# Moving the other weights and inputs behind the first query product of an attention and mixture-of-experts layer, and sharing its tail with GpSimd

## The chip, the core and the metric

The kernel runs on one core of one Trainium2 chip, as one launch. The metric is the device time of an execution in microseconds (us). Before the change, six runs have a median of 538.36 us (535.7 to 539.39). The engines have these names here: PE (TensorE, matrix products), DVE (VectorE), ACT (ScalarE), POOL (GpSimd), SP (SyncE, which here only issues DMAs). ACT and POOL issue DMAs as well. PE and DVE work from and into SBUF, and into PSUM banks, of which there are eight.

## The reference

The input is x, 8 sequences of 512 tokens of 128 numbers, all in fp32. One layer of attention and one of experts are computed, each with a residual and a layer norm behind it:

```python
Q = x @ Wq.T + bq;  K = x @ Wk.T + bk;  V = x @ Wv.T + bv        # 16 heads of 8
scores = einsum('bnqd,bnkd->bnqk', Q, K) / sqrt(128), causal
attn = softmax(scores);  out = (attn @ V) @ Wo.T + bo
x = layernorm(x + out)
probs = softmax(x @ gate_w.T)                                    # 14 experts
w, i = top_2(probs);  w = w / sum(w)
moe = sum over the two: w * (gelu(x @ w1[i] + b1[i]) @ w2[i] + b2[i])
x = layernorm(x + clip(x + moe, -100, 100))
```

## The kernel before, in words

**Loads and constants (lines 90 to 216).** ACT issues the four projection weights (L92), then the query and key biases in eight small DMAs, 32 numbers each (L106), then the value and output bias, the gate, b1, b2 and six rows of -1 for the key tiles (L109 to L208). SP issues all eight sequences of x, 256 KB each (L95). POOL writes the constants: the identity, masks, counters, the value buffers `v_aug` (2 x 128x2048 zeros, L196), `w_all`. DVE casts the counters to fp32 (L166).

**Small products (L293 to L324).** PE turns the four weights, the gate, the value bias and b1 over; DVE copies them to SBUF. From them come the output bias with the value bias folded in (`bo_bc`), and the gate folded into the value and output weights (`wvX`, `woX`), with its bias and sum.

**Attention as a pipeline of steps.** A sequence has four units of four heads, a unit has five steps. In step s, `front` makes a block of 1024 scores on PE and DVE takes its row maxima (L463, L468, L475); `back`, twelve steps behind (LAG), makes the scores again with the maximum taken off, ACT takes their exponential, POOL or PE masks them, and `product` multiplies by the values. Scores use the bf16 pieces of q and k (three pieces each), which `split` makes: a product on PE, a piece on ACT, the rest on DVE (`qrest`, `krest`), the other pieces, a store to DRAM, and `load_rows` reads them back into a ring of tiles. Three PSUM tiles (`ps_u`) hold scores; the other products share two banks (`ps_m`) in order of use.

All other work hangs in a list by step: `at(step, fn, ...)`. Within a step the order is back, front, then the list in the order in which it was filled. Each engine carries out its instructions in the program's order. Sequence b starts at step 20(b - 1): `load_xT` (x turned over), five and six steps later `split` for q and k, fifteen later `values` (L347). What would lie before step 0 stands in step -1: for sequence 0 these are `load_xT`, both splits, `values` and four `load_rows`.

**Routing and experts.** Tokens are scattered by expert to DRAM (`XS`), the experts' blocks run through PE, and their rows are scattered to `OS`. `biases` puts the first terms, b2 by routing weight and the residual y, into `acc` (which is x_sb).

**The tail (L1242 to L1294).** For each of eight chunks (four tiles of 128 tokens) `gather` loads both experts' rows from OS (one DMA on SP, one on ACT, six chunks ahead); `add_up` adds acc and the two by three products with the identity into one of the two `ps_m` banks; `residual_2` on DVE clips (L1263), adds y (L1264) and takes each tile's mean and variance (L220, L221, eight instructions); `layernorm_scale` on POOL makes the scale by a power (L228 to L231); `store`, two chunks later, applies scale and shift in four ACT instructions and issues one DMA on SP.

Of the kernel before, what the change touches and what calls it, by code (L numbers as in the profile page):

```python
# [8 lines left out]
FP = mybir.dt.float32  # L9
AF = mybir.ActivationFunctionType  # L10
ALU = mybir.AluOpType
# [25 lines left out]
def kernel(  # L37
# [56 lines left out]
    for b in range(B):  # L94
        nc.sync.dma_start(x_sb[:, b * NQ : (b + 1) * NQ, :], x_v[:, b * NQ : (b + 1) * NQ, :])  # L95

    ident = const.tile([P, P], FP, tag="ident", name="ident")
    make_identity(nc, ident)

    bias_q = const.tile([P, 1], FP, tag="bias_q", name="bias_q")  # L100
    bias_k = const.tile([P, 1], FP, tag="bias_k", name="bias_k")
    with nc.allow_non_contiguous_dma(reason="128 biases, one to a partition"):
        for src, dst in ((bq, bias_q), (bk, bias_k)):
            src_v = src.rearrange("(g j d) -> g d j", j=GH, d=HD)
            for g in range(NG):
                nc.scalar.dma_start(dst[g * P // NG : (g + 1) * P // NG], src_v[g])  # L106
    bv_bc = const.tile([P, D], FP, tag="bv_bc", name="bv_bc")
    bo_bc = const.tile([P, D], FP, tag="bo_bc", name="bo_bc")
    nc.scalar.dma_start(bv_bc, bv.partition_broadcast(P))  # L109
    nc.scalar.dma_start(bo_bc, bo.partition_broadcast(P))  # L110

    gate_nat = const.tile([E, D], FP, tag="gate_nat", name="gate_nat")
    nc.scalar.dma_start(gate_nat, gate_w)
    b1_nat = const.tile([E * NFC, P], FP, tag="b1_nat", name="b1_nat")
    nc.scalar.dma_start(b1_nat, b1.rearrange("e (c f) -> (e c) f", f=P))
    b2_blk = const.tile([P, NQ, D], FP, tag="b2_blk", name="b2_blk")
    nc.gpsimd.memset(b2_blk, 0.0)
    for t in range(NQ):
        nc.scalar.dma_start(b2_blk[HS * t : HS * t + E, t, :], b2)
# [41 lines left out]

    def counting(name, shape, pattern, base, mult):
        raw = const.tile([P] + shape, I32, tag=f"{name}_i", name=f"{name}_i")
        nc.gpsimd.iota(raw, pattern=pattern, base=base, channel_multiplier=mult)
        dst = const.tile([P] + shape, FP, tag=name, name=name)
        nc.vector.tensor_copy(dst, raw)  # L166
        return dst
# [8 lines left out]
    nc.vector.tensor_copy(place, base_e)  # L176
# [16 lines left out]
    v_aug, qr, kr = [], [], []  # L193
    for i in range(2):
        va = const.tile([P, NQ, HEADS, HS], FP, tag=f"v_aug{i}", name=f"v_aug{i}")
        nc.gpsimd.memset(va, 0.0)  # L196
        nc.gpsimd.memset(va[:, :, :, HD : HD + 1], 1.0)
        v_aug.append(va)
    minus = const.tile([PC, GH, T], BF, tag="minus", name="minus")
    nc.vector.memset(minus, -1.0)  # L200


    ring = const.tile([P, RING, 2, GH, T], BF, tag="ring", name="ring")
    for i in range(RING):
        at = (i - NU % RING) % RING
        qr.append(ring[0:KS, at, 0])
        kr.append(ring[0:KS, at, 1])
        nc.scalar.dma_start(kr[i][KR:KS], minus)  # L208
# [4 lines left out]
    nc.gpsimd.tensor_copy(y_sb[:, :, D + 1], ids[:, 0, :])  # L213
    stats = const.tile([P, NT, 2], FP, tag="stats", name="stats")
    w_all = const.tile([P, NT, HS], FP, tag="w_all", name="w_all")
    nc.gpsimd.memset(w_all, 0.0)

# [55 lines left out]
    with tc.tile_pool(name="work", bufs=2) as work, tc.tile_pool(  # L273
# [20 lines left out]
        for i in range(4):  # L294
            nc.tensor.transpose(wt[:, i * P : (i + 1) * P], wnat[:, i, :], ident)
        for i, dst in enumerate((wqT, wkT)):

            nc.vector.tensor_copy(
                dst.rearrange("p (g d j) -> p g d j", j=GH, d=HD),
                wt[:, i * P : (i + 1) * P].rearrange("p (g j d) -> p g d j", j=GH, d=HD),  # L300
            )
        for i, dst in ((2, wvT), (3, woT)):
            nc.vector.tensor_copy(dst, wt[:, i * P : (i + 1) * P])
        gt = bank("gt")
        nc.tensor.transpose(gt[:, 0:E], gate_nat, ident[:E, :E])
        nc.vector.tensor_copy(gateT, gt[:, 0:E])

        bo_t = bank("bo_t")
        nc.tensor.transpose(bo_t[:, 0:P], bv_bc, ident)
        bvT = work.tile([P, T], FP, tag="num", name="bvT")[:, 0:P]  # L310
        nc.vector.tensor_copy(bvT, bo_t[:, 0:P])
        nc.tensor.matmul(bo_t[:, P : 2 * P], bvT, woT, start=True, stop=True)
        nc.vector.tensor_tensor(bo_bc, bo_bc, bo_t[:, P : 2 * P], ALU.add)
        nc.tensor.transpose(bo_t[:, 2 * P : 3 * P], bo_bc, ident)
        boT = work.tile([P, T], FP, tag="num", name="boT")[:, 0:P]
        nc.vector.tensor_copy(boT, bo_t[:, 2 * P : 3 * P])
        gp = bank("gp")
        for i, w in enumerate((wnat[:, 3, :], boT, ones)):
            nc.tensor.matmul(gp[:, i * P : i * P + E], w, gateT, start=True, stop=True)
        for i, dst in enumerate((woX[:, D:], gate_bias, gate_sum)):  # L320
            nc.vector.tensor_copy(dst, gp[:, i * P : i * P + E])
        bt = bank("bt")
        nc.tensor.transpose(bt[:, 0 : E * NFC], b1_nat, ident[: E * NFC, : E * NFC])
        nc.vector.tensor_copy(b1T, bt[:, 0 : E * NFC])  # L324
# [655 lines left out]
        for b in range(B):  # L980

            s0 = (b - 1) * BSTEP
            at(max(s0, -1), load_xT, b)
            for n, (w, bias, nm) in enumerate(((wqT, bias_q, "q"), (wkT, bias_k, "k"))):
                step = max(s0 + 5 + n, -1)
                at(step, split, step, b, w, bias, nm)
            at(max(s0 + 15, -1), values, b)
            for g in range(NG):
                u = b * NG + g


                at(max(step_of(u - RING, UN) + LAG, s0 + (10, 13, 15, 18)[g], -1), load_rows, u)
# [260 lines left out]

        def add_up(c):
            sums[c] = bank(f"sum_{c}").rearrange("p (t d) -> p t d", d=D)
            parts = acc[:, c * NQ : (c + 1) * NQ, :], *got.pop(c)
            for i, part in enumerate(parts):
                nc.tensor.matmul(sums[c], ident, part, start=(i == 0), stop=(i == 2))

        def residual_2(c):  # L1260
            ts = slice(c * NQ, (c + 1) * NQ)
            z = z_sb[:, ts, :]
            nc.vector.tensor_scalar(z, sums.pop(c), CLIP, -CLIP, ALU.min, ALU.max)  # L1263
            nc.vector.tensor_tensor(z, z, y_sb[:, ts, 0:D], ALU.add)  # L1264
            for i in range(NQ):
                layernorm_stats(ffn, z_sb[:, c * NQ + i, :], c * NQ + i)
            scales[c] = layernorm_scale(ffn, c, 1)

        def store(c):
            rstd, shift = scales.pop(c)  # L1270
            for i in range(NQ):
                t = c * NQ + i
                nc.scalar.activation(
                    z_sb[:, t, :],
                    z_sb[:, t, :],
                    AF.Identity,
                    bias=shift[:, i : i + 1],
                    scale=rstd[:, i : i + 1],
                )
            ts = slice(c * NQ, (c + 1) * NQ)  # L1280
            nc.sync.dma_start(out_v[:, ts, :], z_sb[:, ts, :])

        inner.close()
        ffn = inner.enter_context(tc.tile_pool(name="tail", bufs=3, reuse_waits="tile"))
        for c in range(6):
            gather(c)
        for c in range(B + 2):
            if c < B:
                add_up(c)
                residual_2(c)  # L1290
                if c + 6 < B:
                    gather(c + 6)
            if c >= 2:
                store(c - 2)  # L1294

# [42 lines left out]
```

## Time and profile before

| | us |
|---|---|
| median of six runs | 538.36 |
| profiled execution, device time | 539.48 |
| its span, first to last instruction | 537.8 |
| first query product starts | 20.22 |
| first scores start | 36.07 |
| last expert product ends | about 491.4 |
| first gather issued / first sum with it starts | 498.40 / 502.12 |
| last statistics end / last ACT instruction ends | 530.83 / 534.51 |

Over the span PE is busy 84%, DVE 71%, POOL 60%, ACT 57%; the mean granted PE clock is 0.944 of full speed.

The profile has several views. The page gives busy shares and the costliest groups of instructions. The *timeline* lists instructions in order of time: start, length, engine, line of the kernel, operation, output <- inputs with their shapes, and in brackets how long the engine was idle before and who released it. The *chain of waits* starts from the last instruction and goes back at each step to what released it: start, length, what. The *windows* give the busy time of each engine, the granted PE clock and the DMA rate in stretches of time.

### The profile page before, as it was taken

To read this page: it belongs to the slowest core of one execution; us is meant where nothing else is said; L and a number is where in the kernel's file an instruction comes from. 1 tells how busy PE (TensorE), PEld (TensorE's weight loads), DVE (VectorE), ACT (ScalarE), POOL (GpSimd) and SP (SyncE) were. 2 spreads that over 40 slices of the span, in tenths; PEclk is the share of its full clock that TensorE was granted. 3 is DMA by queue.
4 is the path that set the end of the run, shared out by engine and by line. 5 is a ranking of instruction groups with operands and counts; after the bars stand their busy time and mean duration, and the time that the engine had idled before them with its cause. 6 is when DMAs were issued, how large, how long until landed. Compare 5 with 4: busy or idle time off the path is not lost.

```text
span 537.8 us, 10861 instructions
## 1 busy us (share of the span) xinstructions
PE 449.2 (84%) x3367; PEld 277.2 (52%) x3367; DVE 379.9 (71%) x932; ACT 306.9 (57%) x512; POOL 322.8 (60%) x678
## 2 busy tenths in 40 slices
PE   1737999999999999989999988959867999886690
PEld 0424555555555555545555554526656887774240
DVE  4219668669879878878878889982576665663394
ACT  0302567667766866866866756556554465572054
POOL 6001334453588578578578578676477777777143
PEclk9968699999999999999999999998988999999696
DMA  7144322442443443553443433345155333331952
GB/s 188 36 140 126 104 97 100 135 148 98 141 158 132 141 158 103 153 166 132 143 152 131 142 107 100 101 125 141 34 163 152 107 94 89 89 96 33 243 149 78
DMA packets 66740, 66.23 MB, mean 123 GB/s; under 512 B 10861, under 2 KB 55382, under 8 KB 66683
## 3 DMA queue, kind: packets, MB, share of 16 engines
q1 hardware_dynamic: 55008, 53.26, 33.4%
q0 software_dynamic: 4512, 8.47, 4.7%
q10 hardware_dynamic: 7162, 3.81, 2.6%
q8 instruction: 27, 0.44, 0.4%
q14 instruction: 31, 0.25, 0.2%
HBM read 37.75 MB, written 26.05 MB: 119 GB/s over the span
## 4 chain that ended last, share of the span: by engine, by line
PE 49%; DVE 17%; ACT 11%; POOL 8%; issue 7%; DMA 6%; ACTq 1%; SPq 1%; POOLq 0%; DVEq 0%
PE av L587 12%; PE f L423 7%; PE b L509 7%; ACT pt L563 6%; PE h L1102 5%; PE o L1119 5%; PE f L433 3%; POOL pt L520 3%; DVE mx L463 2%; ACT oT L597 2%; POOL OS L243 2%; DVE mx L468 2%; POOL XS L243 2%; PE bp L1177 1%; DVE ob L1127 1%
## 5 line engine op out<-in xcount | busy, mean ns | idle before, releaser
L563 ACT ACTIVATE pt<-b 128x1024 f32<-128x1024 f32 x160 | 163.0, 1021 | 42.4 <-PE b L509 34.9
L520 POOL TENSOR_SCALAR_AFFINE_SELECT pt<-pt 128x256 f32<-128x256 f32 (+1 forms) x210 | 91.2, 450 | 72.9 <-ACT pt L563 72.2
L423 PE MATMUL f<-ring 72*128 72x384 bf16 (+3 forms) x512 | 114.4, 307 | 18.0 <-DMA ring<-qsc 9.4
L509 PE MATMUL b<-ring 75*128 75x384 bf16 (+3 forms) x512 | 100.7, 308 | 6.2 <-ACT pt L563 3.4
L475 DVE TENSOR_REDUCE mx<-f 128x2 f32<-128x1024 f32 x64 | 78.1, 1223 | 29.0 <-PE f L433 27.9
L243 POOL DMA_INDIRECT OS<-ob,bto_i x77 | 75.1, 975 | 28.7 <-DVE ob L1127 9.7
L587 PE MATMUL av<-pt,v_aug 128*32 128x512 f32 (+3 forms) x1024 | 84.0, 439 | 5.6 <-POOL pt L520 4.9
L433 PE MATMUL f<-causal_bf,ident_bf 128*128 128x256 bf16 (+1 forms) x320 | 82.6, 258 | 0.0
L468 DVE TENSOR_REDUCE mx<-f 128x8 f32<-128x1024 f32 x64 | 77.1, 1213 | 5.5 <-PE f L433 5.2
L423 PEld LDWEIGHTS <-ring 72*128 72x128 bf16 x512 | 50.7, 100 | 52.0 <-issue 28.3
L509 PEld LDWEIGHTS <-ring 75*128 75x128 bf16 x512 | 42.5, 100 | 39.4 <-issue 26.4
L1107 ACT ACTIVATE hT<-h,wt 128x256 f32<-128x256 f32 (+1 forms) x92 | 35.3, 437 | 35.3 <-PE h L1102 35.1
L587 PEld LDWEIGHTS av<-pt,v_aug 128*32 128x32 f32 x1024 | 27.2, 109 | 52.2 <-issue 37.2
L463 DVE TENSOR_REDUCE mx<-f 128x4 f32<-128x1024 f32 x32 | 39.1, 1222 | 14.5 <-PE f L433 12.2
L1102 PE MATMUL h<-bxT,wt 128*128 128x256 f32 (+1 forms) x184 | 44.1, 365 | 5.5 <-DVE begins L873 3.2
L1119 PE MATMUL o<-wt,hT 128*128 128x128 f32 x308 | 44.0, 284 | 1.3 <-ACT hT L1107 1.3
L1119 PEld LDWEIGHTS o<-wt,hT 128*128 128x128 f32 x308 | 42.2, 199 | 4.2 <-ACT hT L1107 2.1
L433 PEld LDWEIGHTS <-ident_bf 128*128 128x128 bf16 x320 | 31.8, 99 | 14.8 <-issue 2.3
L1127 DVE TENSOR_SCALAR ob<-o,bxb 128x128 f32<-128x128 f32 x77 | 24.0, 347 | 20.3 <-PE o L1119 18.1
L243 POOL DMA_INDIRECT XS<-second,to_i x32 | 32.6, 1020 | 8.9 <-issue 8.9
L243 POOL DMA_INDIRECT XS<-y_sb,to_i x32 | 32.3, 1010 | 9.4 <-issue 5.3
L1102 PEld LDWEIGHTS h<-bxT,wt 128*128 128x128 f32 x184 | 30.5, 199 | 11.1 <-ACT wt L1074 5.2
(215 smaller groups left out, 625.0 us busy)
## 6 DMA issues: line engine op xcount, KB each, us to landing
ring<-ksc SPq DMA_DIRECT2D x32, 288.0 KB
ring<-qsc SPq DMA_DIRECT2D x96, 96.0 KB
osc<-oT SPq DMA_DIRECT2D x24, 256.0 KB
bxb<-XS SPq DMA_DIRECT2D x31, 130.0 KB
ring<-in_L_ffn_w_dram SPq DMA_DIRECT2D x28, 128.0 KB
qsc<-qpc SPq DMA_DIRECT2D x24, 128.0 KB
ksc<-kpc SPq DMA_DIRECT2D x24, 128.0 KB
x_sb<-in_L_attn_x_dram SPq DMA_DIRECT2D x8, 256.0 KB
```

The costliest lines, as they stand in the source:

```text
L243: inst = nc.gpsimd.indirect_dma_start(dst, bass.IndirectOffsetOnAxis(ap=idx, axis=0), src, None, bounds_check=bound, oob_is_err=False,)
L423: nc.tensor.matmul(ps[:, col : col + W], qr[u % RING][0:KR, j, qb * P : (qb + 1) * P], kr[u % RING][0:KR, j, :W], start=first, stop=False, ...
L433: nc.tensor.matmul(out, ident_bf, causal_bf[:, 0:n, :], start=False, stop=True, skip_group_check=True,)
L463: nc.vector.reduce_max(mx[:, :, 5], ps.rearrange("p b (s k) -> p (b s) k", s=2), axis=AX.X)
L468: nc.vector.reduce_max(mx[:, j : j + 2, 1:5], ps.rearrange("p b (s k) -> p b s k", k=P), axis=AX.X,)
L475: nc.vector.reduce_max(mx[:, j : j + 2, 7], ps, axis=AX.X)
L509: nc.tensor.matmul(ps[:, col : col + W], kr[u % RING][:, j, kb * P : (kb + 1) * P], qr[u % RING][:, j, kb * P :], start=first, stop=True, ...
L520: nc.gpsimd.affine_select(out=view, in_=view, pattern=[[0, k] for k in n] + [[1, P]], compare_op=ALU.is_ge, fill=0.0, base=0, channel_mult ...
L563: nc.scalar.activation(pt, ps, AF.Exp, scale=SCALE)
L587: nc.tensor.matmul(avs[u][HS * j : HS * (j + 1), kb * P :], v_aug[b % 2][:, kb, g * GH + j, :], p, start=(kb == 0), stop=(kb == 2),)
L1102: nc.tensor.matmul(hp[:, f, :], wt[:, f * P : (f + 1) * P], xT, start=True, stop=True)
L1119: nc.tensor.matmul(op[:, s, :], hT[:, f, s * P : (s + 1) * P], wt[:, F + f * D : F + (f + 1) * D], start=(f == 0), stop=(f == NFC - 1),)
```

## The change

At the front:
- On SP, only the first sequence of x is loaded at once (`load_x(0)`); behind it stand the eight bias DMAs, moved from ACT; then `load_x(1)`. The other six are issued in the pipeline, sequence b + 1 in step 20(b - 1) + 8.
- ACT's other loads (value and output bias, gate, b1, the six rows of -1, b2) go into `load_rest`, step -1, behind both splits.
- The turning of Wv, Wo, the gate and the biases and all products from them become the generator `other_weights`, whose four parts run in steps 1 to 4. Their PSUM tiles are packed in four banks instead of five.
- The counters' casts and copies (`count`) go to step 2. The value products of sequence 0 go from step -1 to step 5.
- POOL's memsets of `v_aug` and DVE's of `minus` come right behind the identity; that of `b2_blk` comes last.

In the tail:
- The sums have six banks of their own (`ps_t`, those that the experts left). `begin_sum` puts the product of acc (the first term) ahead: for chunks 0 to 5 right behind their gathers, for chunks 6 and 7 behind the clips of chunks 0 and 1, whose banks they take.
- The residual is added on POOL, but for the last chunk.
- Statistics run one chunk later (`measure`), with the variance plus epsilon now on DVE and only the power on POOL; the shift is one DVE instruction (`move`), after the next clip.
- In the last chunk DVE normalises two tiles and ACT two, and each half has its own store, on SP and on ACT.

The diff, cut to its core:

```diff
+    def load_x(b):
         nc.sync.dma_start(x_sb[:, b * NQ : (b + 1) * NQ, :], x_v[:, b * NQ : (b + 1) * NQ, :])
+    load_x(0)
...
             for g in range(NG):
-                nc.scalar.dma_start(dst[g * P // NG : (g + 1) * P // NG], src_v[g])
+                nc.sync.dma_start(dst[g * P // NG : (g + 1) * P // NG], src_v[g])
+    load_x(1)
...
+    def load_rest():
+        nc.scalar.dma_start(bv_bc, bv.partition_broadcast(P))
+        nc.scalar.dma_start(bo_bc, bo.partition_broadcast(P))
+        nc.scalar.dma_start(gate_nat, gate_w)
+        nc.scalar.dma_start(b1_nat, b1.rearrange("e (c f) -> (e c) f", f=P))
+        for k in kr:
+            nc.scalar.dma_start(k[KR:KS], minus)
+        for t in range(NQ):
+            nc.scalar.dma_start(b2_blk[HS * t : HS * t + E, t, :], b2)
...
+        def other_weights():
+            wt = bank("wt_2")
+            for i in range(2):
+                nc.tensor.transpose(wt[:, i * P : (i + 1) * P], wnat[:, 2 + i, :], ident)
+            nc.tensor.transpose(wt[:, 2 * P : 2 * P + E], gate_nat, ident[:E, :E])
+            nc.tensor.transpose(wt[:, 3 * P :], bv_bc, ident)
...
+            for dst, src in ((wvT, ...), (woT, ...), (gateT, ...), (bvT, ...)):
+                nc.vector.tensor_copy(dst, src)
+            yield
+            bo_t = bank("bo_t")
+            nc.tensor.matmul(bo_t[:, 0:P], bvT, woT, start=True, stop=True)
+            nc.tensor.transpose(bo_t[:, P : P + E * NFC], b1_nat, ident[: E * NFC, : E * NFC])
+            nc.vector.tensor_tensor(bo_bc, bo_bc, bo_t[:, 0:P], ALU.add)
+            nc.vector.tensor_copy(b1T, bo_t[:, P : P + E * NFC])
+            yield
+            bo_t = bank("bo_t_2")
+            nc.tensor.transpose(bo_t[:, 0:P], bo_bc, ident)
+            nc.vector.tensor_copy(boT, bo_t[:, 0:P])
+            yield
+            gp = bank("gp")
+            for i, w in enumerate((wnat[:, 3, :], boT, ones)):
+                nc.tensor.matmul(gp[:, i * P : i * P + E], w, gateT, start=True, stop=True)
+            for i, dst in enumerate((woX[:, D:], gate_bias, gate_sum)):
+                nc.vector.tensor_copy(dst, gp[:, i * P : i * P + E])
...
-            at(max(s0 + 15, -1), values, b)
+            if b == 0:
+                at(-1, load_rest)
+                others = other_weights()
+                for n in range(1, 5):
+                    at(n, next, others, None)
+                at(2, count)
+            elif b < B - 1:
+                at(s0 + 8, load_x, b + 1)
+            at(max(s0 + 15, 5), values, b)
...
+        def begin_sum(c):
+            sums[c] = ps_t.tile([P, NQ, D], FP, tag="sum", name=f"sum_{c}")
+            nc.tensor.matmul(
+                sums[c], ident, acc[:, c * NQ : (c + 1) * NQ, :], start=True, stop=False
+            )
         def add_up(c):
-            parts = acc[:, c * NQ : (c + 1) * NQ, :], *got.pop(c)
-            for i, part in enumerate(parts):
-                nc.tensor.matmul(sums[c], ident, part, start=(i == 0), stop=(i == 2))
+            for i, part in enumerate(got.pop(c)):
+                nc.tensor.matmul(sums[c], ident, part, start=False, stop=(i == 1))
+        def clip(c):
             nc.vector.tensor_scalar(z, sums.pop(c), CLIP, -CLIP, ALU.min, ALU.max)
-            nc.vector.tensor_tensor(z, z, y_sb[:, ts, 0:D], ALU.add)
+            if c < B - 1:
+                nc.gpsimd.tensor_tensor(z, z, y_sb[:, ts, 0:D], ALU.add)
+        def measure(c):
+            if c == B - 1:
+                nc.vector.tensor_tensor(z, z, y_sb[:, ts, 0:D], ALU.add)
             for i in range(NQ):
                 layernorm_stats(ffn, z_sb[:, c * NQ + i, :], c * NQ + i)
-            scales[c] = layernorm_scale(ffn, c, 1)
+            nc.vector.tensor_scalar(rstd, stats[:, ts, 1], LN_EPS, 1.0, ALU.add, ALU.mult)
+            nc.gpsimd.tensor_tensor(rstd, rstd, power, ALU.pow)
+        def move(c):
+            nc.vector.scalar_tensor_tensor(
+                shift, stats[:, ts, 0], -1.0, scales[c], op0=ALU.mult, op1=ALU.mult
+            )
...
         for c in range(6):
             gather(c)
+            begin_sum(c)
         for c in range(B + 2):
             if c < B:
                 add_up(c)
-                residual_2(c)
+                clip(c)
                 if c + 6 < B:
                     gather(c + 6)
-            if c >= 2:
+                    begin_sum(c + 6)
+            if c == B:
+                measure(c - 1)
+            if c > 1:
+                move(c - 2)
                 store(c - 2)
+            if 1 <= c < B:
+                measure(c - 1)
```

## Prediction

> **What bounds the kernel now.** I read the chain of waits for the start, the timeline for the tail, then the windows for the clock. The change touches only these two ends and twelve or so steps behind the start. First the chain, from the first load to the first reductions (start, length, what):
>
> ```profile
> 1.84 4.31 DMA wnat<-in_L_attn_Wv_dram
> ...
> 10.80 3.02 DMA gate_nat<-in_L_ffn_gate_w_dram
> ...
> 18.43 1.13 PE xt L336 x4
> 19.56 0.02 issue
> 19.58 0.59 ACT xT L338
> 20.18 0.04 issue
> 20.22 2.09 PE q L372 x2
> ...
> 39.69 2.37 DVE mx L468 x2
> 42.05 0.02 issue
> 42.08 0.17 DVE mx L477
> 42.24 2.26 DVE mx L475 x2
> ```
>
> The first query product starts at 20.22 because loads that it doesn't need (the gate's, landed at 13.81) and small products made from them stand before it. The first scores start at 36.07, 15.85 us later. From 39.69 to 51.9 the chain lies on VectorE (DVE): what is added to DVE there is paid in full.
>
> Then the tail, one chunk of eight in the timeline (start, length, engine, line):
>
> ```profile
> 515.61 0.66 DVE L1263 TENSOR_SCALAR x_sb<-sum 128x512 f32<-128x512 f32 x1
> ...
> 516.05 1.01 POOL L229 TENSOR_TENSOR rstd<-rstd,power 128x4 f32<-128x4 f32 x1
> ...
> 516.30 0.69 DVE L1264 TENSOR_TENSOR x_sb<-x_sb,y_sb 128x512 f32<-128x512 f32 x1
> ```
>
> DVE is the bound: the chain has clip 0.59, residual 0.70 and four pairs of statistics 1.70 per chunk, 3.03 in all (the clip of the next starts at 518.63). The slow power on GpSimd (POOL) lies beneath it.
>
> **Front: what goes.** The query product now needs Wq, Wk, the first sequence and the biases. Wk's transpose ran at 5.43; until then 0.97 MB had moved (the half-microsecond windows from 2.0 on), where now 0.51 MB is asked for, which the same windows had moved by 4.0. So Wk and x land between 4.0 and 5.4; I take 4.4. Then 0.48 (transpose), 1.12 (four transposes of x), 0.59 (copy) and hops: the query product at 6.7, ends 6.2 to 7.8. Gain 13.5.
>
> **Front: up to the first scores.** The 15.85 us stay: query product, two splits, stores and ring loads are the same rows. The value products move out, but the chain didn't hold them. New beside it:
> - SP: eight bias issues behind x(0), 0.72 apart as on ACT: 1.3 to 7.0. Those of q land about 7.1, wanted at 8.8 (6.7 + 2.11); those of k, with the gate's 3.02 us from issue, at 9.3 to 10.0, wanted at 10.8. Behind them the second x load, issued by 7.4; the first store stands at 9.5. Cost 0, cover about a microsecond.
> - ACT: fourteen issues (0.46 + 0.44 + 0.45 + 0.37 + 4.37 + 1.64 = 7.7 us) behind the last split, 13.0 to 20.8; the next ACT work comes after the first scores. Hidden there; but they run beside SP's ring loads. An x issue took 0.37 alone and up to 0.51 beside ACT's issues: 0 to 1.5, I take 0.5.
> - POOL: the value buffers' memsets (3.55) now come right after the identity; what follows still ends by 10. The DVE casts that they held for 3.86 (L166) now stand in step 2. The copy of the row numbers into y_sb goes to an idle POOL in step 2. The copies of the weights read PSUM and ran unheld beside POOL's memset at 8.39 (0.28).
>
> First scores at 23.1, 13.0 earlier.
>
> **Steps 1 to 5: what comes back.** DVE gets four copies (0.20 start to start, the gate's 0.10): 0.7; bias sum 0.29, b1 0.10, five small casts and copies 0.55; boT 0.29; three copies at 0.08. Sum 2.2, all in the DVE-bound stretch. PE's transposes and products fit beside the 1.2 us reductions. In step 5 the value products stand before the next query product: 0.49 per half, ACT's copies 0.37 + 0.19, whose bank the query product takes, then 0.9 and 0.69. DVE's qrest can start 2.7 after the scores instead of behind the 1.2 us reduction: DVE idles 1.5 more. Together 3.7; ends 2.2 (idle hidden) and 7 (those products at half clock, as at 61.73 to 63.83). Net of the front: 13.0 - 3.7 = **9.3 earlier**. The six later x loads (0.37 of issue, 256 KB, twelve steps ahead, 16 DMA engines a third busy) I cost at 0; late, one would hold a transpose by its flight, some 3 us.
>
> **Tail: what it brings.** The first terms of chunks 0 to 5 run behind the last expert product: 12 passes at 0.43 = 5.2, from 491.9 to 497.1, under PE's idle 9.87. But those of chunks 6 and 7 wait for the clips of chunks 0 and 1 to free a bank, and on PE the sums of chunks 1 and 2 are queued behind them. Clip 0 ends at 506.6 as before; then six passes, as before. With the clock as it was (0.50 until about 507.4) clip 1 comes at 509.8 (before: 509.51) and clip 2 at X = 513.3. If the 1.1 us pause starts the warming again, X = 514.9; if the early passes keep the clock up, 510.7. I take X = **514.0**.
>
> The clock in the windows is 0.69 over 496 to 500 and 0.50 from 500 on, and PE had stopped at 492.25. The Trainium skill (TensorE: Matmul & The Clock Gate, Part 1: The HAM clock gate) says that the clock falls after an idle window of about 3.4 us and rises after a busy one, windows running freely. An idle of 5.0 and a broken 3.4 would then more often be cold: X = 514.9, 0.9 worse than my sum.
>
> From there each chunk on DVE is clip, shift (move), statistics, rstd. Let t be the end of rstd. POOL starts the power at t + 0.16 and ends at t + 1.2. DVE clips until t + 0.64 and then **waits for the power**: behind the waiting move stand the nine instructions of the statistics, the next clip, and ACT's store. And POOL has the next residual add ready. That kind of instruction (128x512, two SBUF inputs) and what it does to DVE is in the timeline at 333:
>
> ```profile
> 333.82 1.27 POOL L675 TENSOR_TENSOR xb<-x_sb,bo_bc 128x512 f32<-128x512 f32 x1
> 333.84 1.33 DVE L770 TENSOR_TENSOR hot<-rank,best 128x56 f32<-128x56 f32 x1
> ```
>
> The DVE instruction, 0.22 elsewhere, started 0.02 behind POOL's and lasted until POOL's was over. In the tail POOL's add follows its power without a gap (free successors start 0.06 before the end, as at 150.77 and 150.90), while DVE starts 0.03 after a POOL result (150.37). So the add is first and move, with two SBUF inputs, is held to t + 2.42. Then statistics 1.6 and rstd 0.2 (a 128x14 tensor_scalar: 0.17): **4.25 per chunk against 3.03**. Move unheld would give 1.25 + 0.1 + 1.8 = 3.2; these are the two ends, and I take 4.25 because the nearest row is held.
>
> The Trainium skill (GPSIMD Engine Reference, 8. Key points) says that GpSimd and VectorE share SBUF interfaces and contend where the DVE instruction has two SBUF inputs or a 2-port mode. Taken of every POOL instruction that is too much: the 0.69 add at 516.30 lay inside the 1.01 power and took what it takes alone (506.67). By the rule alone the last chunk's DVE add would be held by the power as well, about 0.4 more.
>
> Sum: chunk 2 done at X + 2.55; chunks 3 to 7, 5 x 4.25 = 21.25; last add and statistics 0.72 + 1.8; power 1.2; move 0.15; two ACT halves 0.95 (DVE does the others beside): X + 28.6 = 542.6 against 534.5. Two half-size last stores, 0 to 0.6 quicker, 0.3 taken. The tail **loses 7.8**; ends 2 (unheld, clock as before; below nothing, a gain of 0.5, with the clock up) and 9.
>
> **Total** -9.3 + 7.8 = -1.5 of the profiled execution (539.48; span 537.8, 1.7 around it): 538.0. The median of the runs shown is 1.1 lower, so I forecast 536.9, rounded to **537.0**. A difference under 0.3% (1.6 us) can't be told from none.
>
> **The rivals.**
> - *DVE gets in first.* If move wins its 0.1 us against POOL's add, the period is 3.2, 5.3 less over five chunks: net -6.8, 531.6. For it: at 333.13 a DVE instruction got in between two POOL selects. Against: 333.84, and 341.93, where a cast 0.05 behind a POOL start took 0.36 instead of 0.17.
> - *Slower: the clock in the steps behind the start.* The windows show 0.50 from 50.4 to 64, with PE on the chain from 51.9. There DVE kept PE idle 1.6 us and the clock fell. More DVE work in steps 1 to 5 lengthens such idle. If PE is at half clock on the path for 10 us more, that costs 5: 542. It decides from 3.1 us lost (1.5 + 1.6), some 6 us more of half clock. Against: the added fp32 products keep PE busier, and the next value products raised the clock at 64.
> - *The front does not do what it says.* The query product starts early, but the key biases, last on SP, land late, or ring loads crawl beside ACT's fourteen issues: 2 to 3 of the 13 go, 539.5.
>
> **How the numbers follow.** Forecast 0.58 (its own range 534 to 540: faster 0.27, same 0.25, slower 0.06); DVE first 0.20 (faster); clock 0.15 (slower); front 0.07 (same 0.05, slower 0.02). Faster 0.47, same 0.30, slower 0.23. The range, 530.5 to 541.0, leaves out the far ends of the second and third case.
>
> **What would show it.** First scores at 22 to 24.5; ACT's issues over before them; the reduction of the second unit's first block 13 - 3.7 earlier than 44.42, about 35.3 or less. In the tail: clips 4.2 apart from chunk 3 on, the shift on DVE 1.2 long instead of 0.15, right behind a POOL add of 1.26. Clips 3.2 apart say that DVE got in first; under 3.0 that the wait for the power isn't there and my tail is wrong. A query product after 9, or a gap before the key pieces, says that the loads weren't what held it.

## The result, and the profile after

The changed kernel takes 544.34 us (median of 20 runs, 540.0 to 548.04) against 539.12 for the kernel before (46 runs beside them). The ratio is 1.0102 (95% interval 1.0081 to 1.0123): it is **slower by 1%**, 5.2 us, where 537.0 and a gain of 1.5 us were forecast. The time lies outside the range and on the other side. The profiled execution of after took 542.63 us (span 540.8), 3.0 more span than before's 537.8: some 2 us of the 5.2 are not in the two profiles that are compared below.

Five marks cut the span into stages: the first scores (the first product into f), the 128x4 reduction of the third and of the last unit (there is one such reduction for each unit, L463 before and L489 after), and the first sum that waits for gathered rows (L1296 after). In microseconds:

| | first scores at | to the third unit | third to last unit | tail, from the first sum |
|---|---|---|---|---|
| before | 36.07 | 16.8 | 289.3 | 35.6 |
| after | 23.49 | 20.5 | 293.1 | 44.5 |
| forecast for after | 23.1 | 20.5 | 289.3 | 43.4 |

What lies between these stages (the planner, the experts, the wait for the gathers) is 0.7 shorter after. So the profile says: 12.6 won at the start, 3.7 given back at once as forecast, **3.8 lost in the pipeline, where nothing was expected**, 8.9 lost in the tail.

The chain of waits after, for the same stretch as before's (start, length, what):

```profile
0.80 2.82 DMA wnat<-in_L_attn_Wq_dram
...
6.58 2.09 PE q L398 x2
...
13.61 3.33 DMA ksc<-kpc
...
17.01 4.60 DMA ring<-ksc
...
22.44 1.07 DMA ring<-qsc
```

The chain now begins with the load of Wq, and no small product stands before the query product. Further on, the same view shows what is new:

```profile
97.72 0.79 SPq L432
98.55 0.68 SPq L439
99.27 0.66 SPq L439
99.97 0.65 SPq L439
100.67 3.58 DMA ring<-mt
...
180.34 3.22 DMA ring<-mt
```

The load of a unit's shifted rows (ring<-mt) is on the chain, and SP's issues stand ahead of it. In the list of TensorE's waits the same shows as a sum (in total, times, longest):

```profile
PE b L535 <- DMA ring<-mt: 5.2, 4, 1.9
```

Before, this wait came once, for 1.5 us. The tail after, from the timeline (start, length, engine and line); the first three lines are one chunk, the fourth is the shift that no POOL add meets:

```profile
512.41 1.02 POOL L1317 TENSOR_TENSOR rstd<-rstd,power 128x4 f32<-128x4 f32 x1 [0.69 <-DVE rstd L1314]
513.40 1.18 POOL L1304 TENSOR_TENSOR x_sb<-x_sb,y_sb 128x512 f32<-128x512 f32 x1
513.46 1.14 DVE L1323 SCALAR_TENSOR_TENSOR shift<-stats,rstd 128x4 f32<-128x4 f32 x1 [0.54 <-POOL rstd L1317]
...
530.17 0.16 DVE L1323 SCALAR_TENSOR_TENSOR shift<-stats,rstd 128x4 f32<-128x4 f32 x1 [0.61 <-POOL rstd L1317]
```

A shift of four numbers to a partition takes 1.14 us when it starts 0.06 behind POOL's add and lasts until that add is over, and 0.16 without it: the forecast's mechanism. The clips come 4.08 to 4.21 apart, before 3.03.

### The profile page after: what moved, and what is told of

The parts are those of the page before. It is cut to its first block, busy times and chain, and to the rows that moved or that the text cites. A ratio compares the mean times of both kernels' runs of the same rounds, so it can differ in the third digit from the quotient of the medians.

```text
span 540.8 us, 10856 instructions
## 1 busy us (share of the span) xinstructions
PE 450.5 (83%) x3367; PEld 276.1 (51%) x3367; DVE 378.2 (70%) x943; ACT 306.4 (57%) x510; POOL 326.3 (60%) x661
## 4 chain that ended last, share of the span: by engine, by line
PE 54%; DVE 14%; ACT 12%; DMA 7%; issue 6%; POOL 5%; SPq 1%; POOLq 0%; DVEq 0%; ACTq 0%
PE av L613 13%; PE b L535 8%; PE f L449 8%; ACT pt L589 6%; PE h L1136 5%; PE o L1153 5%; PE f L459 3%; DMA ring<-mt 2%; POOL OS L257 2%; ACT oT L623 2%; ACT x_sb L1339 2%; PE sum L1296 2%; PE bp L1211 1%; DVE mx L494 1%; PE q L398 1%
## 5 line engine op out<-in xcount | busy, mean ns | idle before, releaser
L501 DVE TENSOR_REDUCE mx<-f 128x2 f32<-128x1024 f32 x64 | 78.2, 1223 | 31.7 <-PE f L459 31.7
L613 PE MATMUL av<-pt,v_aug 128*32 128x512 f32 (+3 forms) x1024 | 85.2, 447 | 4.9 <-POOL pt L546 4.5
L1141 ACT ACTIVATE hT<-h,wt 128x256 f32<-128x256 f32 (+1 forms) x92 | 35.4, 438 | 35.2 <-PE h L1136 35.1
L489 DVE TENSOR_REDUCE mx<-f 128x4 f32<-128x1024 f32 x32 | 39.1, 1222 | 15.9 <-PE f L459 13.2
```

Of the source, the lines that this page charges most:

```text
L489: nc.vector.reduce_max(mx[:, :, 5], ps.rearrange("p b (s k) -> p (b s) k", s=2), axis=AX.X)
L501: nc.vector.reduce_max(mx[:, j : j + 2, 7], ps, axis=AX.X)
L613: nc.tensor.matmul(avs[u][HS * j : HS * (j + 1), kb * P :], v_aug[b % 2][:, kb, g * GH + j, :], p, start=(kb == 0), stop=(kb == 2),)
```

## The experiments

Ratios are to the kernel before on the same chip, with 95% intervals. On the chips of e5 to e8 and of e16 and e17 the experts' stage takes 144 to 151 us instead of 114 and the kernel before about 579.7, so between chips only ratios and the stages above are compared. Unit means: the 128x4 reductions as in the table. The first theory was: the start gains what was forecast, the tail loses it again by held shifts, and the later x loads, which I had costed at nothing, are what made the rest. The rival: the faster start is given back in the pipeline whatever the loads do.

### The two ends alone: e1, e2

e1 has before's tail, e2 before's front.

> The changed front with the tail of before. Theory: the front brings 8.9 us until the first value product and the six x loads on SP take 3.0 of it back in the pipeline, so the tail starts 5.9 earlier than in before and ends as it did there: 5.9 us below before, about 533.2, ratio 0.989. Rival: the changed kernel's loss has its seat in the front and the pipeline (its median lies 5.2 above before, its profiled execution only 3.1), then this one is at 536 to 539, ratio 0.995 to 1.0.

> The front of before with the changed tail. Theory: from the first sum that waits for a gather to the end 44.5 us as in the changed kernel against 35.7: 8.9 us above before, about 548, ratio 1.0165, with DVE's shift 1.14 long behind POOL's add in four chunks. Rival: the tail is that slow only because PE's clock fell at that point; with another phase of the clock it loses 5 to 6, 544.5, ratio 1.010.

Measured: e1 ratio 1.0021 (0.9989 to 1.0053), first scores at 23.41, then 23.5, 298.5 and a tail of 35.8. e2 ratio 1.016 (1.0107 to 1.0213), tail 44.2, both as expected; e1's theory (0.989) is out. So the tail costs what the profile said, and **the front by itself brings nothing**: of 12.7 won, 6.7 go before the third unit and 9.2 in the pipeline behind.

### The later x loads: e4, e7, e8, e12, e15, e17

```diff
-    load_x(1)                            # e4: all in front
+    for b in range(1, B):
+        load_x(b)
...
-                at(s0 + 8, load_x, b + 1)
+                at(s0 + 4, load_x, b + 1)    # e7 (on e1), e17 (on after)
+                at(b // 3, load_x, b + 1)    # e15 (on e9, below)
+                at(s0 + 8, load_scrap, b)    # e12: e7 and 2 KB that nothing reads
```

e8 is e1 with these loads issued by POOL.

> The changed kernel, with the six later x loads on SP right behind the biases, as early as before had them but behind what the first product needs; no x load in the pipeline. Theory: the 3.0 us that the pipeline gives back between the first value product and the tail come from these loads standing between SP's stores; without them the distance to before stays at 8.9 until the tail, 3.0 less than the changed kernel, about 541.3, ratio 1.004, and the chain waits for the shift rows at most once. Rival one: the clock's phase or chance makes those waits, 544, ratio 1.010. Rival two: 1.5 MB ahead of the first stores delay the first scores by 2 to 3 us, which eats it: 544, but with first scores at 26 instead of 23.5.

> The changed front with the tail of before, with each later x load four steps earlier, where SP waits for the first query piece and has nothing to issue, instead of between the key pieces' stores. Theory: what the pipeline gives back (8.6 us between the third unit and the last in the profile of that kernel, 3.8 in the changed one) comes from SP's order: the load's 0.7 of issue and its 256 KB ahead of the last stores make every ring load and shift row behind them about 1 us late. In the gap at most 2 of it are left: 5 below the kernel with the loads between the stores (1.0021), ratio about 0.993, and the waits of PE for the shift rows fall from 9.3 to 3 or less. Rival: it is the 256 KB in the pipeline as such, wherever they are issued: ratio 1.0.

> The changed front with the tail of before, with the six later x loads issued by POOL in the same steps, so that SP's queue holds none of them. The same bytes move at the same time. Theory (order on SP): the waits for the shift rows fall as when the loads stand in the gap, ratio about 0.993 to 0.996 (POOL's issue, about 1 us, stands between selects and costs a little). Rival (bytes): ring loads and stores are late all the same, ratio 1.0 or above.

> The front alone with the later x loads in step 20(b - 1) + 4, and in step 20(b - 1) + 8 a load of 2 KB that nothing reads, on the same queue: SP's issue stands at the place where the changed kernel has its x load, without the 256 KB. If the bytes in front of the last key stores are what makes the ring loads late: the pipeline from the third unit on 289 to 290.5, ratio 0.99. The rival, that SP's issue of 0.4 to 0.6 us at this place holds the loads behind it: 293 to 298, ratio 0.995 to 1.005.

> The kernel with all three edits, but with the six later x loads in steps 0, 1 and 2 (two, three and one) and none in the pipeline behind. If they cost by standing among the key stores: the waits for shifted rows fall to those of before (1.5 us in all against 4.7 in e9), from the third unit to the last 289 to 290, ratio 0.979 to 0.982. The rival, that they then stand in front of the first sequence's ring loads and the second's stores: the third unit comes 1 to 3 later, ratio 0.984 to 0.987.

> The changed kernel with one edit: the six later x loads in step 20(b - 1) + 4 instead of 8. My theory, that this place costs 3 to 7 us: ratio 0.997 to 1.004 against 1.010 for the changed kernel, the pipeline from the third unit to the last 289 to 291.5. The rival, that what e7, e11 and e12 gained over the front alone came with the chip: ratio 1.008 to 1.012, 293 to 298.

| | ratio | first scores | to the third unit | third to last unit | tail |
|---|---|---|---|---|---|
| e4 | 1.005 (1.0019 to 1.0081) | 26.09 | 23.8 | 291.7 | 44.6 |
| e7 | 0.9897 (0.986 to 0.9933) | 23.75 | 22.6 | 289.7 | 35.6 |
| e8 | 0.9984 (0.9947 to 1.0022) | 23.54 | 23.7 | 300.2 | 35.8 |
| e12 | 0.9866 (0.9816 to 0.9916) | 23.58 | 21.6 | 292.6 | 35.6 |
| e15 | 0.9853 (0.9811 to 0.9896) | 23.57 | 22.7 | 291.4 | 32.6 |
| e17 | 0.9985 (0.9956 to 1.0014) | 23.26 | 20.5 | 292.4 | 44.3 |

(The profiled execution of e8 took 5 us more than the median of its runs, so its stages are long.) The six loads four steps sooner are worth 0.0124 in ratio with before's tail (e7 against e1) and 0.0117 in the changed kernel itself (e17 against after): **6.3 to 6.7 us of 539** (with the intervals of the ratios some 4 to 9), from an edit of one digit. e1 and e7 ran on different chips, and the record names no chip for after.

The stages support it but for one profile. From the first scores to the last unit, before takes 306.1. With the new front and late loads on SP, e1, e3, e5 and e6 take 319.2 to 322.0; with the loads elsewhere on SP, the eleven others take 312.4 to 315.6. On one chip it is 321.0 and 319.3 (e5, e6) against 312.4 (e7). But after's own profile has 313.5, no longer than e17's 312.9: the cost that the ratios show is not in it, and its 3.8 lies within the 0.4 to 4.3 that the kernels with moved loads lose in the same stage. And e17's 292.4 from the third unit on is between the theory's 289 to 291.5 and the rival's 293. So the rival holds a part as well: even with the loads moved, 6.3 to 9.5 of the earlier start are given back by the last unit, where 3.7 was forecast.

e17's ratio on the median of 538.36 that the forecast started from makes 537.6; 537.0 was forecast.

How it costs is on SP's queue. After, from the timeline around the load for sequence 3 (issue start, length):

```profile
80.51 0.59 SPq L411 DMA_DIRECT2D ksc<-kpc  x1
81.15 0.59 SPq L96 DMA_DIRECT2D x_sb<-in_L_attn_x_dram  x1
81.84 0.48 SPq L628 DMA_DIRECT2D osc<-oT  x1
82.36 1.22 SPq L411 DMA_DIRECT2D ksc<-kpc  x2
85.65 0.86 SPq L432 DMA_DIRECT2D ring<-ksc  x1
...
88.78 0.78 SPq L522 DMA_DIRECT2D ring<-mt  x1
```

The same place in e7:

```profile
83.05 0.59 SPq L411 DMA_DIRECT2D ksc<-kpc  x1
83.72 0.54 SPq L628 DMA_DIRECT2D osc<-oT  x1
84.33 1.18 SPq L411 DMA_DIRECT2D ksc<-kpc  x2
87.09 0.87 SPq L432 DMA_DIRECT2D ring<-ksc  x1
...
90.17 0.77 SPq L522 DMA_DIRECT2D ring<-mt  x1
```

From the first store of the key pieces to the ring load that waits for them it is 5.14 us after and 4.04 in e7; the load of the shifted rows behind it is as much later (8.27 and 7.12). SP works in order, so one late ring load delays everything behind it. The mean of this stretch over the six sequences splits the cost: before 4.49, after 5.54, e1 5.81, e7 4.34, e15 4.54; with the issue and no bytes (e12) 4.91; with the bytes and no issue of SP's (e8, in its long profile) 5.02. So the issue takes about 0.4 and the 256 KB ahead of the last two stores about as much again: both held a part, and e12's ratio, as good as e7's, says that the issue alone is not seen in the time.

In e8 the waits for shifted rows stayed (7.5 us in all), as its rival had it; its ratio lies between the two, and its stages can't be weighed. e4 has the ratio that its theory gave (1.004), and shows the other price: with all of x in front, first scores come 2.6 later. e15, with none of these loads behind step 2, was to bring the waits for shifted rows down to 1.5 us: they were 3.9 (e9 4.7), and its ratio is its rival's.

### The tail: e3, e5, e6, e10

```diff
+            if 1 <= c < B:               # e3, on after: the shift behind
+                measure(c - 1)           # the next statistics
             if c > 1:
                 move(c - 2)
                 store(c - 2)
-            if 1 <= c < B:
-                measure(c - 1)
...
-                layernorm_stats(ffn, z_sb[:, c * NQ + i, :], c * NQ + i)
+                nc.vector.bn_stats(st, z_sb[:, c * NQ + i, :])   # e5, on after:
+                nc.vector.bn_aggr(mean_var[:, i, 0:2], st)       # a PSUM bank
...
-                shift, stats[:, ts, 0], -1.0, scales[c], op0=ALU.mult, op1=ALU.mult
+                shift, mean_var[:, :, 0], -1.0, scales[c], op0=ALU.mult, op1=ALU.mult
...
                 add_up(c)                # e6, on after: first terms 6 and 7
+                if 1 <= c < B - 5:       # behind sums 1 and 2
+                    begin_sum(c + 5)
                 clip(c)
                 if c + 6 < B:
                     gather(c + 6)
-                    begin_sum(c + 6)
```

e10 is before's front with the edits of e3 and e6.

> The changed kernel, with the shift and the store of a chunk behind the statistics of the next one instead of ahead of them: the power is done by then, and POOL's add nearly so. Nothing else differs. Theory: waiting for the power (0.54 to 0.61) and being held by POOL's add (1.0) make up the period of 4.1 to 4.2 on DVE; without them clip 0.6, statistics and rstd 1.8, shift 0.1 give 2.5: five periods shorter by 1.6, 8 us below the changed kernel, about 536, ratio 0.995. Rival: POOL (add 1.18, power 1.02, gaps) or a hold at another DVE instruction takes over, period 3.2 or more: at most 5 less, 539.5 or above, ratio 1.0.

> The changed kernel, with the last layer norm's means and variances written to a PSUM bank instead of SBUF, so that the shift has one SBUF input (the scale) and one from PSUM. It still waits for the power, and POOL's add still starts ahead of it. Theory: the hold comes from two SBUF inputs, so the shift is 0.15 to 0.2 long again, the period falls from 4.1 to 4.2 to 3.2, four chunks by 1.0: 4 us below the changed kernel, ratio about 1.003. Rival: any DVE instruction that starts behind POOL's add is held, or the wait for the power is what sets the period: shift 1.1 long or period unchanged, ratio 1.010.

> The changed kernel, with the first terms of chunks 6 and 7 behind the sums of chunks 1 and 2 on PE, so that PE has nothing to wait for. Theory: PE runs through from the first sum on, its clock rises sooner, clip 1 comes 7.3 after the first sum instead of 9.9 and clip 2 about 10 instead of 13.5: 3 to 3.5 us below the changed kernel, ratio 1.004. Rival: the clock stays low as long as before and DVE's statistics of chunk 0, behind clip 1, set clip 2: 1 us or less, ratio 1.008.

> The front of before with the changed tail, whose shift stands behind the next statistics and whose first terms 6 and 7 stand behind the sums of chunks 1 and 2. My theory: tail 34 to 35 against 35.7, ratio 0.996 to 1.000 (0 to 2 us under before). The rival, that early first terms bring nothing once the shift is out of the way: tail 37, ratio 1.002 to 1.004.

Measured tails: e3 **37.3** (after 44.5), e5 38.0, e6 41.9, e10 33.1 (before 35.6). Ratios: e3 1.0008 (0.9969 to 1.0047), e5 1.0111 (1.0058 to 1.0164), e6 1.0147 (1.0089 to 1.0205), e10 0.9976 (0.9942 to 1.0009). The tails of e3, e5 and e6 are 7.2, 6.5 and 2.6 shorter than after's (some 8, 4 and 3 to 3.5 expected), but the ratios are those of their rivals or above: 0.995, 1.003 and 1.004 were expected. They carry the late x loads, as after does, but their profiles took 5.7 to 7.5 longer than after's from the first scores to the last unit (above). e6's six runs spread from 578.54 to 592.01, so its ratio settles nothing. In e5 the shift reads its means from PSUM, so it has one SBUF input left. Its timeline at the place where after shows 1.14:

```profile
558.70 1.18 POOL L1304 TENSOR_TENSOR x_sb<-x_sb,y_sb 128x512 f32<-128x512 f32 x1
558.76 0.16 DVE L1327 SCALAR_TENSOR_TENSOR shift<-mv,rstd 128x4 f32<-128x4 f32 x1 [0.54 <-POOL rstd L1321]
```

The same instruction, 0.06 behind the same add, is not held, and the clips come 3.1 to 3.23 apart (3.2 was the forecast's figure for an unheld move): 3.9 of the tail's 6.5 less; the rest came before clip 2. So for this instruction the hold comes from its two SBUF inputs. The Trainium skill (GPSIMD Engine Reference, 8. Key points) names that condition, "contention with DVE instructions in a 2-port perf mode or with two SBUF inputs"; e5's 0.16 against 1.14 agrees with it. Two inputs are not all that can meet a hold: in before, the casts of L166, with one input, took up to 3.86 beside POOL's memsets. e3 takes the wait away without moving the data:

```profile
518.10 0.17 DVE L1314 TENSOR_SCALAR rstd<-stats 128x4 f32<-128x4 f32 x1
518.18 0.15 DVE L1323 SCALAR_TENSOR_TENSOR shift<-stats,rstd 128x4 f32<-128x4 f32 x1
518.25 0.68 DVE L1301 TENSOR_SCALAR x_sb<-sum 128x512 f32<-128x512 f32 x1
```

With 1.7 us of statistics between the power's request and the shift, the power is there when the shift comes to its turn, and the period falls to 2.54: under before's 3.03, which is what POOL's add was to bring. e6 brings clips 1 and 2 3.2 and 4.2 sooner, but one more shift is held, so 2.6 are left. In e10 the two edits together make the changed tail 2.5 shorter than before's, more than forecast, since the clock opens sooner as well (below).

### The start: e11, e13, e14, e16, e18, and all mended, e9

```diff
+            at(max(s0 + 15, 9), values, b)   # e11, on e7; 5 in after
...
+        def warm_up(n):                      # e13: 18, e14: 8, e16: 30, on e9
+            wm = unit("warm")                # e18: 30, on e15
+            for i in range(n):
+                nc.tensor.matmul(wm[:, i % 2, 0 : 2 * P], ident,
+                                 xTs[0][:, 0 : 2 * P], start=True, stop=True)
...
+                at(-1, warm_up, n)
                 at(-1, load_rest)
```

e9 is after with the edits of e3, e6 and e7. The products of warm_up are read by nothing.

> The changed kernel with three edits: the later x loads in step 20(b - 1) + 4, the shift behind the next chunk's statistics, the first terms of chunks 6 and 7 behind the sums of chunks 1 and 2. My theory: three separate losses, each mended. First scores at 23.5 (12.6 sooner), 4 to 6 of it given back up to the third unit; the pipeline from there 289 to 290.5, as before; the tail 34 to 35, since the period of 2.54 is under the 3.03 of before and clips 1 and 2 come some 3 sooner than with the shift alone moved: 7 to 10 us under before, ratio 0.981 to 0.988. The rival, that the tail is then bound by TensorE at half clock, as its sums stand: tail 37, 5 us under before, ratio 0.99.

> The front alone with the later x loads in step 20(b - 1) + 4 and the value products of sequence 0 in step 9 instead of 5. My theory, that the value products at half clock and VectorE's wait behind them are a part of the 6 us given back in the first steps: from the first scores to the third unit 20 to 21.5 instead of 22.6, ratio 0.985 to 0.988 against 0.99 with the values in step 5. The rival, that TensorE's half clock alone sets these steps: 22.6 again, or the loss moves to the steps behind, ratio 0.99.

> The kernel with all three edits (e9), and ahead of load_rest 18 products of 128x256 in fp32 that nothing reads: they fill TensorE's idle time from 10.4 to the first scores. My theory, that the half clock is what the first steps lose: the clock opens before the first scores, these start at 23 to 24, the third unit comes 17 to 19 later instead of 23.8 (before: 16.8), ratio 0.971 to 0.977 against 0.982 for e9. The rival, that VectorE's added work and the value products in step 5 lose it whatever the clock is: 22 to 24 from the first scores to the third unit, ratio 0.982 or more, and if the products outlast the ring loads the first scores come up to 4 later.

> The same with 8 such products: TensorE is busy from 10.4 to 16 or 17 and then idle until the first scores at 23. If TensorE must be busy right up to the scores for its clock to stay open: the clock falls again by 20, the third unit comes 20 to 24 behind the first scores, as in e9 or as in after, ratio 0.977 to 0.982. The rival, that one opening before is enough for the next to come after 4 us of work, as in after: 19.5 to 21, ratio 0.975 to 0.977.

> As e13, with 30 products, which at 0.44 each last from 10 to 23 or 24. My theory: the clock is open at the first scores and stays so, the first scores start at 23 to 24.5, the third unit comes 17 to 19 later instead of 22.7 to 23.8, ratio 0.971 to 0.979. The rival, that the clock falls in these steps all the same or that VectorE's added work sets them: 21 or more, ratio 0.984 or more.

> The kernel with the shift behind the next statistics and the first terms 6 and 7 behind sums 1 and 2, the six later x loads in steps 0 to 2 and 30 products that nothing reads ahead of the first scores. My theory, that the rest of the loss in the pipeline is the x loads': third unit 20 to 20.5 behind the first scores, from there to the last 289.3 to 291.3, ratio 0.976 to 0.981. The rival, that what the start gains is given back in the pipeline whatever the loads do: 293 to 294 from the third unit on, ratio 0.984 to 0.987.

| | ratio | first scores | to the third unit | third to last unit | tail |
|---|---|---|---|---|---|
| e9 | **0.9822** (0.9777 to 0.9868) | 22.83 | 23.8 | 290.8 | 31.8 |
| e11 | 0.9871 (0.9833 to 0.9908) | 23.05 | 22.8 | 291.1 | 35.2 |
| e13 | 0.9874 (0.9835 to 0.9913) | 23.38 | 22.7 | 292.9 | 31.7 |
| e14 | 0.9858 (0.9814 to 0.9903) | 23.5 | 23.7 | 290.4 | 31.8 |
| e16 | 0.9853 (0.9815 to 0.989) | 23.5 | 20.2 | 293.6 | 32.9 |
| e18 | **0.9819** (0.9781 to 0.9857) | 24.06 | 20.2 | 292.2 | 32.7 |

e9 beats both kernels: 531.11 against 540.21 on its chip. Its ratio is the expected one, but by errors that cancel: 7.0 are given back up to the third unit (4 to 6 expected), and the tail is 31.8 (34 to 35 expected). None of the five kernels below it in the table, nor e15, can be told from it by their intervals.

Why do the first steps take 22 to 24 us in most kernels and 20.5 in the profile of after? The timeline's length of one kind of product (two of 72x384) is the clock: 0.63 at half, 0.38 open. In e1:

```profile
38.55 0.63 PE L449 MATMUL f<-ring 72*128 72x384 bf16 x2
...
40.42 0.38 PE L449 MATMUL f<-ring 72*128 72x384 bf16 x2
```

In after:

```profile
26.22 0.63 PE L449 MATMUL f<-ring 72*128 72x384 bf16 x2
...
27.90 0.38 PE L449 MATMUL f<-ring 72*128 72x384 bf16 x2
```

Both start their scores at 23.4 and 23.5. In after the clock opened 4.4 us later, in e1 15.8 later, with TensorE shown busy all that time. In the 15 profiles with the new front whose clock was down at the first scores, the first recorded rise came 3.5 to 4.4 behind them in four (after, e3, e12, e17) and 13.6 to 16.4 in eleven. In e3 and e12 the clock fell again at 30.5 and 34.0 and the third unit came 22.6 and 21.6 behind the first scores; in after and e17 it stayed open until 41.5 and 40.9, and it was 20.5.

The record tells the four from the eleven. In each profile all recorded changes of the clock lie a whole multiple of 3.41 us apart (after: 14.24, 27.89, 41.55, 55.20). Where a point of this grid fell 0.1 to 1.0 us behind the first scores, the clock opened at the next point, in four of four; where the first point fell 1.8 to 3.4 behind, it stayed shut for three or four points more, in eleven of eleven. So the profile of after, with its 3.7, is the lucky kind; which work keeps the clock shut is not shown. e16's 30 products fill the wait from 10.29 until the scores, and the clock is open at the first of them:

```profile
24.59 0.38 PE L456 MATMUL f<-ring 72*128 72x384 bf16 x2
```

The third unit then comes 20.2 behind the scores instead of e9's 23.8. So of the 7.0 that e9 gives back here, by these two profiles **3.6 are the clock and 3.4 are DVE's added work and idle time**, for which 3.7 was forecast (e16's clock was down once more, from 31.3 to 34.7). My 17 to 19 for e16 and e13 was too low: I had let the clock pay for all of it, and e16's ratio is its rival's. e13 didn't try it (the clock opened beneath its products, they ended at 17.9, and it fell before the scores); e14 the same, and its ratio missed. e11's rival held: the place of the value products makes no difference to the third unit (22.8 against 22.6), and its ratio can't be told from e7's.

The 3.6 are not seen in the time: e16 loses 4.3 in the pipeline (waits for shifted rows: 5.1 us), e18 2.9. e18 was to tell whether the x loads take it back; 292.2 is between the theory's 291.3 and the rival's 293, and the ratio just outside both. It loses 4.5 at one unit, the eighteenth, with no x load in the pipeline. What takes that part back isn't settled.

## Why the prediction was wrong, point by point

- **The front's start** was right: query product at 6.58 (6.7 forecast), first scores at 23.49 (23.1). ACT's fourteen issues took 12.25 to 24.31, not 13.0 to 20.8, and so ended 0.8 behind the first scores; ACT's next work came at 25.82.
- **Steps 1 to 5 take back 3.7**: the profile of after shows 3.7, and e16, with the clock open for most of it, 3.4. In most other profiles it is 5.8 to 7.0, so that the agreement is luck in part. My upper end of 7 with "those products at half clock" and the rival of the clock held this, but I put the half clock into step 5 and behind, while it stands over all steps from the first scores on.
- **"The six later x loads I cost at 0" is the step that failed.** By the ratios it cost 6.3 to 6.7 us, though after's own profile does not show it (above). I looked at what the load's own reader needs (twelve steps ahead) and at the mean load of the DMA engines (a third, I wrote; the windows from the third unit to the last show 0.42 before and 0.43 after), and not at what is queued behind it on SP: two key stores, the ring loads that wait for them, and the shifted rows that TensorE waits for some ten us later. My price for the case that they are late was a transpose waiting for x; it was a neighbour that waited.
- **"Net of the front 9.3 earlier"** let what is won at the third unit stand up to the tail. No kernel with the new front keeps it: with the loads moved, the stage from the third unit to the last still takes 0.4 to 4.3 more than before's 289.3. What takes this back stays open.
- **The tail loses 7.8**: 8.9. The held shift is as forecast (1.14, period 4.15 against 4.25). Four shifts are held, not five, since the last chunk's add is on DVE: from clip 2 on it took 27.6, not 28.6. But clip 2 itself came 13.5 behind the first sum, not 11.9. TensorE paused 0.78 twice, for clips 0 and 1, and its clock stayed at half longer. The windows after from the first sum on (busy TensorE and its count, granted clock, DMA share, GB/s):

```profile
496.26:498.26 2.00, 2.00 (x3) 0.50 1.20 299
498.26:500.26 2.00, 1.78 (x3) 0.50 1.20 291
500.26:502.26 2.00, 1.44 (x2) 0.50 1.21 291
502.26:504.26 2.00, 2.00 (x3) 0.50 1.20 290
504.26:506.26 2.00, 1.84 (x3) 0.63 1.20 290
506.26:508.26 2.00, 1.38 (x3) 1.00 1.20 290
```

  In e9, where the first terms of chunks 6 and 7 wait for nothing, there is no pause, and the clock opens 3.1 behind the first sum instead of 9.5:

```profile
496.91:498.91 2.00, 2.00 (x3) 0.50 1.18 305
498.91:500.91 2.00, 2.00 (x5) 0.73 1.19 291
500.91:502.91 2.00, 2.00 (x6) 1.00 1.20 290
```

  The Trainium skill (TensorE: Matmul & The Clock Gate, Part 1: The HAM clock gate) has the clock rise after one busy window of about 3.4 us. The 3.1 us from the first sum in e9 and the 4.4 at the start of after lie near it; the paused 9.5 us here fit a broken window; the 13.6 to 16.4 us at the start, with TensorE shown busy, do not, and no run here says what the gate saw there. Its value for X would have been 0.9 nearer than mine.
- **The last stores** in two halves brought nothing (3.4 us from the last ACT work to the end of the span, before 3.3), 0.3 was taken.
- **The rivals.** DVE did not get in first: all four shifts that meet an add are held. The front did what it says. The slower case, the clock, named a true loss, but not the one that decides: with the x loads moved and nothing else (e17) the kernel is level with before in time, as forecast. By stages it is not the forecast's sum: its profile has 3.1 more than before's in the pipeline and 8.6 in the tail, and the record has no profile of before on its chip to say where that is made up.

## What to carry to other kernels

A transfer that nobody waits for still has a place in an in-order queue: price it by what is behind it there and by the bytes in front of the next short transfer, not by when its own data is wanted. A wait that joins two engines should have work between request and use: the same shift cost 1.14 right behind its power and 0.15 with the next statistics in between. A gain at the start must be read at the end of the steps behind it: 12.6 us at the first scores were 9 at the third unit and 5 at the last in the profile of after, and in e1, with the tail of before, nothing in the time.

## What was not expected of the hardware

- TensorE's clock took either 3.5 to 4.4 or 13.6 to 16.4 us of work to open, by where its grid of 3.41 us fell, behind 12.4 to 15.7 us of idle (5.5 and 8.6 in e13 and e14).
- A 256 KB load put between 128 KB stores delayed the ring loads behind them by about 1 us (5.54 against 4.49 in the mean), though the 16 DMA engines were 0.43 busy in the mean of that stretch.
- The clock that the windows show is not to be read ahead of its first recorded change: in e1 they show 1.00 from 24 to 40, where the same products take 0.63 that take 0.38 from 40 on.
- POOL's power and POOL's add differ in what they do to a DVE instruction with two SBUF inputs. The add of 1.18 us held one that began 0.06 behind it to its end. Beside the power the 128x512 add took its usual 0.69 after (at 532.12) as before; after, it was the power that took longer, 1.31 instead of 1.02.
